# One-value-a-token rows through DRAM instead of products, in a four-layer graph network on one core

## Chip, cores and metric

One core of a Trainium2 chip runs the whole program in one launch, in float32. The metric is device microseconds of that core; on one core there is no die to compare, and all runs agree within 0.3% of their median, those of the slower kernels within 0.6%, so all are taken as of one state (the fast one). Ratios are the mean time of one kernel's runs over that of the other's of the same rounds, so not quite the ratio of the medians that are quoted. Several chips served; the kernel before took 1639.2 to 1639.6 us (median) on each, so times of different rounds may stand side by side.

## The reference, cut

```python
# x: 64 x 256 x 128, adj: 256 x 256 (one graph for all 64 items)
def layer0(x):                       # _pair_indices cut
    h = x @ others_weight
    u1, u2 = h @ a1, h @ a2          # one value a token each
    e = u1[:, idx1] + u2[:, idx2]    # leaky relu 0.1, masked by adj, softmax over axis 1
    return einsum('bik,bkl->bil', att, h) + x @ self_weight
def layer1(x):
    h = x @ W
    e = leaky_relu((h @ a_src)[:, :, None] + (h @ a_dst)[:, None, :], 0.2)  # masked, softmax over -1
    return elu(attn @ h)
x = layernorm(x + layer0(x)); x = layernorm(x + layer1(x))
x = layernorm(x + gated_5_steps(x, adj)); x = layernorm(x + chebyshev_3(x, adj))   # layers 2 and 3, cut
```

Where layers 0 and 1 need a leaky relu of "value of token i plus value of token j", one of the two must lie along the free axis of every partition: a row of 512 values (two items), the same on all 128 partitions.

## The kernel before

Two items make a unit; 32 units pass through the four layers in five lanes. All instructions are handed over in an order that a small list scheduler makes when the kernel is built; on the chip each engine then goes through its own list strictly in that order.

```python
class Plan:
    LATENCY = {"pe": 220, "dve": 150, "act": 150, "pool": 200, "sp": 3000}   # "sp": the queue of transfers
    OWN = {"pe": 0, "dve": 70, "act": 70, "pool": 100, "sp": 0}
    ...
    def seen_at(self, t, by):        # when task `by` may use what t made
        return t.end if t.eng != by.eng else t.off + self.OWN[t.eng]
    ... # run(): free[e] = t.off = now + t.ns;  t.end = t.off + self.LATENCY[e] + t.wait
```

A transfer is added with ns=450, so it is planned to land 3.45 us after its issue. Layer 0 and layer 1 before, cut:

```python
def layer0(u, L):
    xT = feature_major(u, L)                                  # 4 transposes, copy by ACT
    matmul(ps_c, wc_b, xT)                                    # the row on all partitions: 128x512   (L408)
    ... matmul(ps_d[:, b], xb[:, b, k:N:2], wu[:, k])         # one-column sums, 4                  (L412)
    ... matmul(hx[b], xb[..], wx0)                            # h and self product, 256 columns, 4  (L423)
    ... # Prelu, mask, softmax; h times 1/sum
    ... matmul(hx[b][ic, 1], p[..], h[..])                    # attention times h, 8 of 128 columns (L458)
    layernorm(...)
def layer1(u, L):
    xT = feature_major(u, L)                                  # 4 transposes
    ... matmul(ps_h[b], xb[..], wx1)                          # x W, 129 columns, 4                 (L473)
    matmul(ps_e, ws_b, xT)                                    # the row on all partitions: 128x512   (L477)
    ... # Prelu, exp, mask
    ... matmul(ps_o, p[..], h[..])                            # attention times h, 8 of 130 columns (L504)
```

The softmax here doesn't subtract the row's maximum and nothing guards it: scores larger than these inputs give would overflow.

## Time and profile before

| | kernel before |
|---|---|
| time (median) | 1639.5 us |
| span, granted TensorE clock | 1637.2 us, 0.999 |
| PE / DVE / ACT busy | 99% / 58% / 50% |
| transfers | all loads issued by 37 us; after that only the 32 stores of results |

PE is TensorE's matmuls, PEld its weight loads, DVE VectorE, ACT ScalarE, POOL GpSimd, SP the engine that issues transfers. Where PE is busy 99% of the span and every other engine at 60% or less, time is PE's sum of instructions. The lines that show it are in the prediction below.

### The profile page before, as it was taken

How to read it: one execution, taken by the hardware profiler on the slowest of the kernel's cores; microseconds unless marked ns; L12 is line 12 of the kernel's file. 1: busy time of each engine (PE TensorE's matmuls, PEld its weight loads, DVE VectorE, ACT ScalarE, POOL GpSimd, SP SyncE). 2: the span in 40 equal slices, each digit the busy share in tenths (PEclk: the TensorE clock that was granted, in tenths of full speed). 3: DMA queues.
4: the chain of work that ended last, by engine and by line, in shares of the span. 5: the costliest groups of instructions: out<-in, count | busy, mean ns of one | idle time of the engine just before them, and what ended most of it. 6: DMA issues, size and time to landing. Idle time of an engine off the chain costs nothing.

```text
span 1637.2 us, 18751 instructions
## 1 busy us (share of the span) xinstructions
PE 1615.9 (99%) x6999; PEld 1095.2 (67%) x6999; DVE 950.4 (58%) x2214; ACT 820.2 (50%) x1602; POOL 145.7 (9%) x134
## 2 busy tenths in 40 slices
PE   8899999999999999999999999999999999999998
PEld 7556667666667666676666666667666667765566
DVE  6844556655556655466555665555656556763544
ACT  4644445544554545454455544545545544654542
POOL 0100001100001100011000110001101011100001
PEclk9999999999999999999999999999999999999999
DMA  9000000000000000000000000000000000000000
GB/s 241 1 0 7 7 7 8 7 1 7 7 7 7 7 1 7 7 8 7 1 7 7 7 7 1 7 7 7 7 1 7 7 7 7 7 1 0 1 7 26
DMA packets 36731, 19.42 MB, mean 12 GB/s; under 512 B 2465, under 2 KB 36513, under 8 KB 36641
## 3 DMA queue, kind: packets, MB, share of 16 engines
q1 hardware_dynamic: 36640, 18.23, 4.2%
q8 instruction: 55, 0.90, 0.2%
q14 instruction: 36, 0.29, 0.1%
...
## 4 chain that ended last, share of the span: by engine, by line
PE 94%; DVE 3%; ACT 1%; POOL 0%; issue 0%; DMA 0%; POOLq 0%; DVEq 0%; ACTq 0%
PE ps L543 41%; PE ps L527 20%; PE ps L597 7%; PE ps L570 4%; PE ps L604 3%; PE ps L423 3%; PE ps L375 3%; PE ps L504 3%; PE ps L458 3%; PE ps L408 2%; PE ps L473 2%; PE ps L477 2%; PE ps L412 1%; DVE x L395 1%; DVE st L386 0%; POOL rstd L391 0%
## 5 line engine op out<-in xcount | busy, mean ns | idle before, releaser
L543 PE MATMUL ps<-m,gT 128*128 128x512 f32 x960 | 463.7, 595 | 1.0 <-ACT e L549 0.6
L391 POOL TENSOR_TENSOR rstd<-ve,nhalf 128x4 f32<-128x4 f32 x128 | 145.0, 1134 | 1485.7 <-DVE ve L388 1459.0
L543 PEld LDWEIGHTS ps<-m,gT 128*128 128x128 f32 x960 | 173.1, 190 | 135.3 <-issue 116.2
L527 PE MATMUL ps<-adjT,ht 128*128 128x256 f32 x1024 | 253.6, 381 | 0.5 <-ACT ht L574 0.5
L551 DVE SCALAR_TENSOR_TENSOR e<-e,xT 128x512 f32<-128x512 f32 x160 | 110.3, 690 | 205.0 <-ACT e L549 204.5
L527 PEld LDWEIGHTS ps<-adjT,ht 128*128 128x128 f32 x1024 | 188.1, 190 | 54.9 <-issue 27.4
L562 DVE TENSOR_TENSOR p<-p,xT 128x512 f32<-128x512 f32 x160 | 110.3, 689 | 175.8 <-ACT p L556 175.3
L558 ACT ACTIVATE e<-ps,bias 128x512 f32<-128x512 f32 x160 | 109.9, 687 | 146.6 <-PE ps L543 146.6
L539 ACT COPY m<-ps 128x512 f32<-128x512 f32 x160 | 93.7, 585 | 174.4 <-PE ps L527 168.8
L543 PE MATMUL ps<-xT,gT 128*128 128x512 f32 x320 | 164.2, 595 | 0.5 <-ACT xT L377 0.5
L543 PE MATMUL ps<-e,u5T 128*128 128x512 f32 x320 | 163.0, 597 | 0.9 <-DVE e L551 0.8
L549 ACT ACTIVATE e<-ps,bias 128x512 f32<-128x512 f32 x160 | 109.9, 687 | 106.7 <-PE ps L543 106.0
L527 PE MATMUL ps<-adjT,x 128*128 128x256 f32 x512 | 143.6, 380 | 0.0
L570 PEld LDWEIGHTS ps<-ident,xT 128*128 128x128 f32 x640 | 83.7, 141 | 76.6 <-issue 53.4
L556 ACT ACTIVATE p<-ps,bias 128x512 f32<-128x512 f32 x160 | 109.9, 687 | 35.2 <-PE ps L543 34.8
L574 ACT COPY ht<-ps 128x512 f32<-128x512 f32 x128 | 74.6, 585 | 97.6 <-PE ps L570 96.8
L563 DVE SCALAR_TENSOR_TENSOR p<-e,p 128x512 f32<-128x512 f32 x160 | 110.2, 689 | 21.8 <-ACT e L558 18.7
L570 PE MATMUL ps<-ident,xT 128*128 128x128 f32 x640 | 118.7, 274 | 0.6 <-DVE xT L565 0.4
L395 DVE TENSOR_SCALAR x<-ps,st,rstd 128x128 f32<-128x128 f32 x256 | 93.4, 404 | 41.6 <-POOL rstd L391 41.0
L375 PE MATMUL ps<-ident,x 128*128 128x128 f32 x512 | 112.5, 276 | 1.6 <-DVE x L395 1.1
L377 ACT COPY xT<-ps 128x512 f32<-128x512 f32 x128 | 74.6, 585 | 78.6 <-PE ps L375 78.1
L565 DVE SCALAR_TENSOR_TENSOR xT<-p,xT 128x512 f32<-128x512 f32 x160 | 110.0, 687 | 2.9
(107 smaller groups left out, 2046.4 us busy)
## 6 DMA issues: line engine op xcount, KB each, us to landing
x<-in_x_dram SPq DMA_DIRECT2D x32, 256.0 KB, 5.5
out_dram<-x SPq DMA_DIRECT2D x32, 256.0 KB, 2.3
...
adj_t<-in_adj_dram SPq DMA_DIRECT2D x1, 256.0 KB, 2.6
...
```

Source lines behind the costliest of these rows:

```text
L375: add(PE, 110, lambda g=g: nc.tensor.transpose(ps.ap[:, g * P : (g + 1) * P], X[u].ap[:, g // NC, g % NC, :], ident.ap), (X[u], ident), (ps,))
L391: add(POOL, 1050, lambda: nc.gpsimd.tensor_tensor(rstd.ap, ve.ap, nhalf.ap, op=ALU.pow), (ve, nhalf), (rstd,))
L527: add(PE, mm_ns(N), lambda b=b, mc=mc: nc.tensor.matmul(ps.ap[:, b * N : (b + 1) * N], (src.ap if len(src.ap.shape) == 4 else src.ap.rearr ...
L543: add(PE, mm_ns(T), lambda: nc.tensor.matmul(ps.ap, w(), rhs.ap, start=start, stop=stop, skip_group_check=True), (c, rhs), (ps,))
L549: add(ACT, 600, lambda ps_g=ps_g: nc.scalar.activation(r.ap, ps_g.ap, AF.Tanh, bias=bias2.ap[:, 1:2], scale=0.5), (ps_g, bias2), (r,))
L551: add(DVE, 600, lambda h=h: nc.vector.scalar_tensor_tensor(r.ap, r.ap, 1.0, h.ap, op0=ALU.add, op1=ALU.mult), (r, h), (r,))
L556: add(ACT, 600, lambda ps_v=ps_v: nc.scalar.activation(v.ap, ps_v.ap, AF.Tanh, bias=bias2.ap[:, 2:3]), (ps_v, bias2), (v,))
L562: add(DVE, 600, lambda h=h: nc.vector.tensor_sub(v.ap, v.ap, h.ap), (v, h), (v,))
L563: add(DVE, 600, lambda: nc.vector.scalar_tensor_tensor(v.ap, z.ap, 1.0, v.ap, op0=ALU.add, op1=ALU.mult), (v, z), (v,))
L565: add(DVE, 600, lambda h=h, new=new: nc.vector.scalar_tensor_tensor(new.ap, v.ap, 0.5, h.ap, op0=ALU.mult, op1=ALU.add), (v, h), (new,))
L570: add(PE, 110, lambda g=g, h=h, ps_t=ps_t: nc.tensor.transpose(ps_t.ap[:, g * P : (g + 1) * P], h.ap[:, g * P : (g + 1) * P], ident.ap), ( ...
L597: add(PE, mm_ns(N), lambda k=k, src=src, c=c, b=b: nc.tensor.matmul(view(c)[:, :, b, :], bn(src.ap)[:, b, c * P : (c + 1) * P], w3.ap[:, k ...
```

## The change

Its intent is to take products off PE. In layer 0 the row and the one-column sums come out of the h product as extra columns; in layer 1 both sums come out of layer 0's attention product as extra columns. A column has one value per partition; to turn it into a row on all partitions it is stored to DRAM and loaded back to every partition. Layer 1 multiplies attention by x first, then by W, which spares transposes and half of the products. A sixth lane is to cover the transfers; unit 0 still goes by products.

```diff
-LANES = 5
-LEAD = 20
+LANES = 6
+LEAD = 10
+DIRECT = 1
+    def to_row(row, src, col, n=1):
+        add("sp", 450, lambda: nc.sync.dma_start(
+            row.ap.rearrange("o (g p k) -> (o p) g k", g=G, k=n), src.ap[:, :, col : col + n]), (src,), (row,))
+    def from_row(t, row):
+        add("sp", 450, lambda: nc.sync.dma_start(t.ap, row.ap.rearrange("o n -> (o n)").partition_broadcast(P)), (row,), (t,))
+    def on_all(u, t, row, src, col):
+        if u >= DIRECT:
+            to_row(row, src, col); from_row(t, row); return t
+        ... # else 4 transposes of the column, broadcast
 # layer 0
-        matmul(ps_c, wc_b, xT) ... one-column sums ... h and self product, 256 columns
+        ... h product of 133 columns (h, 2 sums for layer 1, 3 for layer 0), copied early by ACT
+        to_row(L["rowu"], h, D + 2, 2); u4 <- rowu (pairs of tokens); d = u4[:, :, 0] + u4[:, :, 3]
+        row = on_all(u, lc, L["row"], h, D + 4)
+        ... self product (130 columns) and attention times h (130 columns) in one accumulation
 # layer 1
-        feature_major; x W; matmul(ps_e, ws_b, xT); attention times h
+        es = on_all(u, L["m"], L["row"], esd, 0)
+        ... ps_x = x-transposed times attention (4 of 256 columns), then W (4 of 129 columns)
 # cut: folded weights and the layernorm that goes with them, loads of x kept to two per lane, casts of views
```

`row` is 512 values of 4 bytes, `rowu` 512 pairs of 8 bytes. Each value is one piece, since a partition's four values lie apart on both sides.

More of the change, by code (lines that the diff above doesn't have):

```diff
@@ L190 @@
     PE, DVE, ACT, POOL = "pe", "dve", "act", "pool"
+    C0 = D + 5
     const = ctx.enter_context(tc.tile_pool(name="const", bufs=1))
     psum = ctx.enter_context(tc.tile_pool(name="psum", bufs=1, space=bass.MemoryType.PSUM))
+    dram = ctx.enter_context(tc.tile_pool(name="dram", bufs=1, space=bass.MemoryType.DRAM))
     def sb(name, shape):
@@ L217 @@
     out_u = out.rearrange("(u b) (c p) d -> u p b c d", b=UB, p=P)
-    X = {}
+    xs, X = [cell(f"x{k}", [P, UB, NC, D]) for k in range(2 * LANES)], {}
     def load_x(u):
-        X[u] = load(f"x{u}", x_u[u], [P, UB, NC, D], 1000)
-    adj_t = load("adj_t", adj.rearrange("(c p) j -> p c j", p=P), [P, NC, N])
+        X[u] = c = xs[u % len(xs)]
+        add("sp", 1000, lambda: nc.sync.dma_start(c.ap, x_u[u]), (), (c,))
+    w1 = load("w1", W, [D, D])
+    asd = cell("asd", [D, 2])
+    for k, a in enumerate((a_src, a_dst)):
+        add("sp", 450, lambda k=k, a=a: nc.sync.dma_start(asd.ap[:, k : k + 1], a), (), (asd,))
     wo = load("wo", others_weight, [D, D])
@@ L227 @@
     wself = load("wself", self_weight, [D, D])
+    adj_t = load("adj_t", adj.rearrange("(c p) j -> p c j", p=P), [P, NC, N])
     load_x(1)
-    w1 = load("w1", W, [D, D])
-    asd = cell("asd", [D, 2])
-    for k, a in enumerate((a_src, a_dst)):
-        add("sp", 450, lambda k=k, a=a: nc.sync.dma_start(asd.ap[:, k : k + 1], a), (), (asd,))
     load_x(2)
@@ L243 @@
     wk = load("wk", weight_1, [D, D, 7], 1500)
-    for u in range(4, NU):
+    for u in range(4, LANES):
         load_x(u)
@@ L290 @@
     add(DVE, 420, lambda: nc.vector.tensor_scalar(mask1.ap, mask1.ap, 0.0, None, op0=ALU.is_gt), (mask1,), (mask1,))
-    def projected(name, w, vecs):
-        wT = transposed(name + "T", [(w, w.ap)])
-        ps, t = bank(), cell(name, [P, 2])
-        add(PE, 150, lambda: nc.tensor.matmul(ps.ap[:, 0:2], wT.ap[:, 0], vecs.ap, start=True, stop=True),
-            (wT, vecs), (ps,))
-        add(DVE, 150, lambda: nc.vector.tensor_copy(t.ap, ps.ap[:, 0:2]), (ps,), (t,))
-        return t
-    wu = projected("wu", wo, att)
@@ L301 @@
-    wc = cell("wc", [P, 1])
-    add(DVE, 150, lambda: nc.vector.tensor_add(wc.ap, wu.ap[:, 0:1], wu.ap[:, 1:2]), (wu,), (wc,))
-    wc_b = cell("wc_b", [P, P])
-    add(DVE, 230, lambda: nc.vector.tensor_copy(wc_b.ap, wc.ap.to_broadcast([P, P])), (wc,), (wc_b,))
-    wx0 = cell("wx0", [P, 2, D])
-    add(DVE, 150, lambda: nc.vector.tensor_copy(wx0.ap[:, 0], wo.ap), (wo,), (wx0,))
-    add(DVE, 250, lambda: nc.vector.tensor_add(wx0.ap[:, 1], wself.ap, ident.ap), (wself, ident), (wx0,))
-    wsd = projected("wsd", w1, asd)
@@ L311 @@
-    ws_b = cell("ws_b", [P, P])
-    add(DVE, 230, lambda: nc.vector.tensor_copy(ws_b.ap, wsd.ap[:, 0:1].to_broadcast([P, P])), (wsd,), (ws_b,))
-    wx1 = cell("wx1", [P, D + 1])
-    add(DVE, 150, lambda: nc.vector.tensor_copy(wx1.ap[:, 0:D], w1.ap), (w1,), (wx1,))
-    add(DVE, 150, lambda: nc.vector.tensor_copy(wx1.ap[:, D : D + 1], wsd.ap[:, 1:2]), (wsd,), (wx1,))
+    centre = cell("centre", [P, P])
+    add(DVE, 150, lambda: nc.vector.tensor_scalar_add(centre.ap, ident.ap, -1.0 / D), (ident,), (centre,))
@@ new lines, in product @@
+    def product(ps, at, n, lhs, lhs_ap, rhs, rhs_ap):
+        add(PE, mm_ns(n), lambda: nc.tensor.matmul(ps.ap[:, at : at + n], lhs_ap(), rhs_ap(), start=True, stop=True,
+                                                   skip_group_check=True), (lhs, rhs), (ps,))
+    wx1 = cell("wx1", [P, D + 1])
+    w1cT = cell("w1cT", [P, D])
+    ps_w1, ps_w1T = bank(), bank()
+    product(ps_w1T, 0, D, w1, lambda: w1.ap, centre, lambda: centre.ap)
+    add(DVE, 230, lambda: nc.vector.tensor_copy(w1cT.ap, ps_w1T.ap[:, 0:D]), (ps_w1T,), (w1cT,))
@@ new lines @@
+    product(ps_w1, 0, D, centre, lambda: centre.ap, w1, lambda: w1.ap)
+    add(DVE, 230, lambda: nc.vector.tensor_copy(wx1.ap[:, 0:D], ps_w1.ap[:, 0:D]), (ps_w1,), (wx1,))
+    add(DVE, 60, lambda: nc.vector.memset(wx1.ap[:, D : D + 1], 1.0 / D), (), (wx1,))
+    right0 = cell("right0", [P, C0])
+    ps_r = bank()
+    add(DVE, 150, lambda: nc.vector.tensor_copy(right0.ap[:, 0:D], centre.ap), (centre,), (right0,))
+    product(ps_r, 0, 2, w1cT, lambda: w1cT.ap, asd, lambda: asd.ap)
+    add(DVE, 100, lambda: nc.vector.tensor_copy(right0.ap[:, D : D + 2], ps_r.ap[:, 0:2]), (ps_r,), (right0,))
@@ new lines @@
+    add(DVE, 100, lambda: nc.vector.tensor_copy(right0.ap[:, D + 2 : D + 4], att.ap), (att,), (right0,))
+    add(DVE, 100, lambda: nc.vector.tensor_add(right0.ap[:, D + 4 : D + 5], att.ap[:, 0:1], att.ap[:, 1:2]),
+        (att,), (right0,))
+    woT = transposed("woT", [(wo, wo.ap)])
+    add(DVE, 250, lambda: nc.vector.tensor_add(wself.ap, wself.ap, ident.ap), (wself, ident), (wself,))
+    wselfT = transposed("wselfT", [(wself, wself.ap)])
+    wx0, ws0 = cell("wx0", [P, C0]), cell("ws0", [P, D + 2])
@@ L318 @@
+    for t, wT, n in ((wx0, woT, C0), (ws0, wselfT, D + 2)):
+        ps = bank()
+        product(ps, 0, n, wT, lambda wT=wT: wT.ap[:, 0], right0, lambda n=n: right0.ap[:, 0:n])
+        add(DVE, 230, lambda t=t, n=n, ps=ps: nc.vector.tensor_copy(t.ap, ps.ap[:, 0:n]), (ps,), (t,))
     gs = [cell(f"gs{k}", [D, D]) for k in range(3)]
@@ L354, in lane_cells @@
             c[name] = Cell(c[at].ap.rearrange("p g n -> p (g n)")[:, half * T : (half + 1) * T])
-        c["h0"] = cell(f"h0_{k}", [P, G, D])
-        c["h1"] = cell(f"h1_{k}", [P, G, D + 2])
+        c["h0"] = cell(f"h0_{k}", [P, G, C0])
         c |= {name: cell(f"{name}_{k}", [P, G]) for name in ("nm", "s", "rs", "rstd", "ve")}
@@ L359, in lane_cells @@
         c["st"] = cell(f"st_{k}", [P, UB, 6])
-        add(DVE, 60, lambda: nc.vector.memset(c["h1"].ap[:, :, D + 1 : D + 2], 1.0), (), (c["h1"],))
+        c["u"] = cell(f"u_{k}", [P, UB, 4])
+        c["esd"] = cell(f"esd_{k}", [P, G, 2])
+        for name, n in (("row", 1), ("rowu", 2)):
+            c[name] = Cell(dram.tile([1, T * n], F32, tag=f"{name}_{k}", name=f"{name}_{k}"))
         return c
@@ L378, in feature_major, with layernorm @@
         return L[name]
-    def layernorm(u, L, pairs, swap=False):
+    def to_row(row, src, col, n=1):
[5 more added lines that the diff above has]
+        if u >= DIRECT:
+            to_row(row, src, col)
+            from_row(t, row)
+            return t
+        ps = bank()
+        for g in range(G):
+            add(PE, 110, lambda g=g: nc.tensor.transpose(
+                ps.ap[:, g * P : (g + 1) * P], src.ap[:, g, col : col + 1].to_broadcast([P, P]), ident.ap),
+                (src, ident), (ps,))
+        return ps
+    def layernorm(u, L, pairs, swap=False, centred=False):
         st, ve, rstd = L["st"], L["ve"], L["rstd"]
@@ L394, in layernorm @@
                 b, ch = (j, k) if swap else (k, j)
+                if centred:
+                    add(DVE, 260, lambda k=k, j=j, b=b, ch=ch, view=view: nc.vector.tensor_scalar(
+                        X[u].ap[:, b, ch, :], view()[:, j, :], rstd.ap[:, 2 * k + j : 2 * k + j + 1], 1.0,
+                        op0=ALU.mult, op1=ALU.add), (c, rstd), (X[u],))
+                    continue
                 add(DVE, 260, lambda k=k, j=j, b=b, ch=ch, view=view: nc.vector.tensor_scalar(
@@ L406, in layer0 @@
         xb = bn(xT.ap)
-        ps_c, ps_d = bank(), bank()
-        tail = [add(PE, mm_ns(T), lambda: nc.tensor.matmul(ps_c.ap, wc_b.ap, xT.ap, start=True, stop=True),
-                    (xT, wc_b), (ps_c,))]
+        lc, d, e, p, h, u4 = L["m"], L["d"], L["e"], L["p"], L["h0"], L["u"]
+        nm, s, rs = L["nm"], L["s"], L["rs"]
         for b in range(UB):
-            for k in range(2):
-                tail.append(add(PE, 240, lambda b=b, k=k: nc.tensor.matmul(
-                    ps_d.ap[:, b : b + 1], xb[:, b, k : N : 2], wu.ap[:, k : k + 1], start=(k == 0), stop=(k == 1)),
-                    (xT, wu), (ps_d,)))
@@ L416, in layer0 @@
-        hx = [bank() for _ in range(UB)]
-        def hxv(b):
-            return hx[b].ap.rearrange("p (c k d) -> p c k d", c=NC, k=2)
-        for b in range(UB):
-            for c in range(NC):
-                add(PE, mm_ns(N), lambda b=b, c=c: nc.tensor.matmul(
-                    hx[b].ap[:, c * N : (c + 1) * N], xb[:, b, c * P : (c + 1) * P],
-                    wx0.ap.rearrange("p k d -> p (k d)"), start=(c == 0), stop=True, skip_group_check=True),
-                    (xT, wx0), (hx[b],), tail)
@@ L427, in layer0, with hv @@
-        lc, d, nd, e, p = L["m"], L["d"], L["nd"], L["e"], L["p"]
-        nm, s, rs, h = L["nm"], L["s"], L["rs"], L["h0"]
-        add(ACT, 600, lambda: nc.scalar.activation(lc.ap, ps_c.ap, AF.Prelu, alpha=0.1), (ps_c,), (lc,))
-        add(ACT, 160, lambda: nc.scalar.activation(d.ap, ps_d.ap[:, 0:UB], AF.Prelu, alpha=0.1), (ps_d,), (d,))
+            hx = bank()
+            def hv(hx=hx):
+                return hx.ap[:, 0 : NC * C0].rearrange("p (c k) -> p c k", c=NC)
+            for c in range(NC):
+                add(PE, mm_ns(C0), lambda b=b, c=c, hv=hv: nc.tensor.matmul(
+                    hv()[:, c, :], xb[:, b, c * P : (c + 1) * P], wx0.ap, start=(c == 0), stop=True,
+                    skip_group_check=True), (xT, wx0), (hx,))
@@ new lines, in layer0 @@
+            add(ACT, 400, lambda b=b, hv=hv: nc.scalar.copy(h.ap[:, b * NC : (b + 1) * NC, :], hv()), (hx,), (h,))
+        if u >= DIRECT:
+            to_row(L["rowu"], h, D + 2, 2)
+            add("sp", 450, lambda: nc.sync.dma_start(
+                u4.ap, L["rowu"].ap.rearrange("o (b p k) -> (o p) b k", b=UB, p=P)), (L["rowu"],), (u4,))
+            add(DVE, 100, lambda: nc.vector.tensor_add(d.ap, u4.ap[:, :, 0], u4.ap[:, :, 3]), (u4,), (d,))
+            ds = d
+        else:
+            ds = bank()
+            for b in range(UB):
+                for k in range(2):
+                    add(PE, 240, lambda b=b, k=k: nc.tensor.matmul(
+                        ds.ap[:, b : b + 1], xb[:, b, k : N : 2], wx0.ap[:, D + 2 + k : D + 3 + k],
+                        start=(k == 0), stop=(k == 1)), (xT, wx0), (ds,))
@@ L431, in layer0 @@
+        add(ACT, 160, lambda: nc.scalar.activation(d.ap, ds.ap[:, 0:UB], AF.Prelu, alpha=0.1), (ds,), (d,))
+        row = on_all(u, lc, L["row"], h, D + 4)
+        add(ACT, 600, lambda: nc.scalar.activation(lc.ap, row.ap, AF.Prelu, alpha=0.1), (row,), (lc,))
         ev = e.ap.rearrange("p (b c) n -> p b c n", b=UB)
@@ L445, in layer0 @@
         for g in range(G):
-            add(ACT, 620, lambda g=g: nc.scalar.activation(
+            add(ACT, 400, lambda g=g: nc.scalar.activation(
                 p.ap[:, g, :], e.ap[:, g, :], AF.Exp, bias=nm.ap[:, g : g + 1], accum_out=s.ap[:, g : g + 1]),
                 (e, nm), (p, s))
-        add(DVE, 120, lambda: nc.vector.reciprocal(rs.ap, s.ap), (s,), (rs,))
-        for b in range(UB):
-            add(DVE, 350, lambda b=b: nc.vector.tensor_mul(
-                h.ap[:, b * NC : (b + 1) * NC, :], hxv(b)[:, :, 0, :],
-                rs.ap[:, b * NC : (b + 1) * NC].rearrange("p (c o) -> p c o", o=1).to_broadcast([P, NC, D])),
-                (hx[b], rs), (h,))
@@ L455, in layer0, with yv @@
-        for b in range(UB):
+        tail = [add(DVE, 120, lambda: nc.vector.reciprocal(rs.ap, s.ap), (s,), (rs,))]
+        add(DVE, 700, lambda: nc.vector.tensor_mul(
+            h.ap[:, :, 0 : D + 2], h.ap[:, :, 0 : D + 2],
+            rs.ap.rearrange("p (g o) -> p g o", o=1).to_broadcast([P, G, D + 2])), (h, rs), (h,))
+        esd, rstd = L["esd"], L["rstd"]
+        ys = []
+        for b in range(UB):
+            y = bank()
+            def yv(y=y):
+                return y.ap[:, 0 : NC * (D + 2)].rearrange("p (c k) -> p c k", c=NC)
+            ys.append((y, yv))
+            for c in range(NC):
+                add(PE, mm_ns(D + 2), lambda b=b, c=c, yv=yv: nc.tensor.matmul(
+                    yv()[:, c, :], xb[:, b, c * P : (c + 1) * P], ws0.ap, start=(c == 0), stop=False,
+                    skip_group_check=True), (xT, ws0), (y,), tail)
@@ L456, in layer0 @@
             for ic in range(NC):
                 for kc in range(NC):
-                    add(PE, mm_ns(P), lambda b=b, ic=ic, kc=kc: nc.tensor.matmul(
-                        hxv(b)[:, ic, 1, :], p.ap[:, b * NC + kc, ic * P : (ic + 1) * P], h.ap[:, b * NC + kc, :],
-                        start=False, stop=True, skip_group_check=True), (p, h), (hx[b],))
-        layernorm(u, L, [(hx[b], lambda b=b: hxv(b)[:, :, 1, :]) for b in range(UB)])
-    def layer1(u, L):
-        xT = feature_major(u, L)
-        xb = bn(xT.ap)
-        H = D + 2
-        ps_h = [bank() for _ in range(UB)]
-        tail = []
-        for b in range(UB):
-            for c in range(NC):
-                tail.append(add(PE, mm_ns(D + 1), lambda b=b, c=c: nc.tensor.matmul(
-                    ps_h[b].ap[:, c * H : c * H + D + 1], xb[:, b, c * P : (c + 1) * P], wx1.ap,
-                    start=(c == 0), stop=True, skip_group_check=True), (xT, wx1), (ps_h[b],)))
-        ps_e = bank()
-        add(PE, mm_ns(T), lambda: nc.tensor.matmul(ps_e.ap, ws_b.ap, xT.ap, start=True, stop=True),
-            (xT, ws_b), (ps_e,), tail)
-        h, e, p = L["h1"], L["e"], L["p"]
-        for b in range(UB):
-            add(ACT, 300, lambda b=b: nc.scalar.copy(
-                h.ap[:, b * NC : (b + 1) * NC, 0 : D + 1],
-                ps_h[b].ap[:, 0 : NC * H].rearrange("p (c k) -> p c k", c=NC)[:, :, 0 : D + 1]), (ps_h[b],), (h,))
@@ new lines, in layer0 @@
+                    add(PE, mm_ns(D + 2), lambda b=b, ic=ic, kc=kc, yv=yv: nc.tensor.matmul(
+                        yv()[:, ic, :], p.ap[:, b * NC + kc, ic * P : (ic + 1) * P], h.ap[:, b * NC + kc, 0 : D + 2],
+                        start=False, stop=(kc == NC - 1), skip_group_check=True), (p, h), (y,))
+        layernorm(u, L, [(y, lambda yv=yv: yv()[:, :, 0:D]) for y, yv in ys], centred=True)
+        for b, (y, yv) in enumerate(ys):
+            add(DVE, 120, lambda b=b, yv=yv: nc.vector.tensor_mul(
+                esd.ap[:, b * NC : (b + 1) * NC, :], yv()[:, :, D : D + 2],
+                rstd.ap[:, b * NC : (b + 1) * NC].rearrange("p (c o) -> p c o", o=1).to_broadcast([P, NC, 2])),
+                (y, rstd), (esd,))
@@ L484, in layer1 @@
+    def layer1(u, L):
+        H = D + 1
+        esd, e, p = L["esd"], L["e"], L["p"]
+        es = on_all(u, L["m"], L["row"], esd, 0)
         for g in range(G):
@@ L486, in layer1 @@
             add(ACT, 400, lambda g=g, b=b: nc.scalar.activation(
-                e.ap[:, g, :], ps_e.ap[:, b * N : (b + 1) * N], AF.Prelu, bias=h.ap[:, g, D : D + 1], alpha=0.2),
-                (ps_e, h), (e,))
+                e.ap[:, g, :], bn(es.ap)[:, b, :], AF.Prelu, bias=esd.ap[:, g, 1:2], alpha=0.2), (es, esd), (e,))
         ef, pf = e.ap.rearrange("p g n -> p (g n)"), p.ap.rearrange("p g n -> p (g n)")
@@ L493, in layer1 @@
             mask1.ap.rearrange("p (o c) n -> p o (c n)", o=1).to_broadcast([P, UB, NC * N])), (e, mask1), (p,))
+        ps_x, px = bank(), L["xT0"]
+        for b in range(UB):
+            for jc in range(NC):
+                add(PE, mm_ns(N), lambda b=b, jc=jc: nc.tensor.matmul(
+                    ps_x.ap[:, b * N : (b + 1) * N], X[u].ap[:, b, jc, :], p.ap[:, b * NC + jc, :],
+                    start=(b == 0 and jc == 0), stop=(jc == NC - 1), skip_group_check=True), (X[u], p), (ps_x,))
+        add(ACT, 500, lambda: nc.scalar.copy(px.ap, ps_x.ap), (ps_x,), (px,))
         rs, hp, hn, th = L["rs"], L["ht"], L["m"], L["xT1"]
-        ex = Cell(L["h0"].ap.rearrange("p g d -> p (g d)"))
+        ex = L["h0"]
+        exf = ex.ap.rearrange("p g d -> p (g d)")[:, 0:T]
         for b in range(UB):
@@ L502, in layer1 @@
             for ic in range(NC):
-                for jc in range(NC):
-                    add(PE, mm_ns(H), lambda b=b, ic=ic, jc=jc, ov=ov: nc.tensor.matmul(
-                        ov()[:, ic, :], p.ap[:, b * NC + jc, ic * P : (ic + 1) * P], h.ap[:, b * NC + jc, :],
-                        start=(ic == 0 and jc == 0), stop=True, skip_group_check=True), (p, h), (ps_o,))
+                add(PE, mm_ns(H), lambda b=b, ic=ic, ov=ov: nc.tensor.matmul(
+                    ov()[:, ic, :], bn(px.ap)[:, b, ic * P : (ic + 1) * P], wx1.ap,
+                    start=(ic == 0), stop=True, skip_group_check=True), (px, wx1), (ps_o,))
             r = rs.ap[:, b * NC : (b + 1) * NC].rearrange("p (c o) -> p c o", o=1)
-            add(DVE, 120, lambda r=r, ov=ov: nc.vector.reciprocal(r, ov()[:, :, D + 1 : D + 2]), (ps_o,), (rs,))
+            add(DVE, 120, lambda r=r, ov=ov: nc.vector.reciprocal(r, ov()[:, :, D : D + 1]), (ps_o,), (rs,))
             add(DVE, 350, lambda b=b, r=r, ov=ov: nc.vector.tensor_mul(
@@ L513, in layer1 @@
         add(ACT, 550, lambda: nc.scalar.activation(th.ap, hn.ap, AF.Tanh, scale=0.5), (hn,), (th,))
-        add(ACT, 550, lambda: nc.scalar.activation(ex.ap, hn.ap, AF.Exp), (hn,), (ex,))
+        add(ACT, 550, lambda: nc.scalar.activation(exf, hn.ap, AF.Exp), (hn,), (ex,))
         xf = X[u].ap.rearrange("p b c d -> p (b c d)")
@@ L517, in layer1 @@
             (hp, X[u]), (hp,))
-        add(DVE, 600, lambda: nc.vector.scalar_tensor_tensor(th.ap, ex.ap, 1.0, th.ap, op0=ALU.add, op1=ALU.mult),
+        add(DVE, 600, lambda: nc.vector.scalar_tensor_tensor(th.ap, exf, 1.0, th.ap, op0=ALU.add, op1=ALU.mult),
             (ex, th), (th,))
@@ L610, in spawn @@
     def spawn(u, lane):
+        if u + LANES < NU:
+            load_x(u + LANES)
         for layer in (layer0, layer1, layer2, layer3):
```

## The prediction

> **What bounds the kernel now.** I read the page first, its busy table and its chain that ended last.
>
> ```profile
> PE 1615.9 (99%) x6999; PEld 1095.2 (67%) x6999; DVE 950.4 (58%) x2214; ACT 820.2 (50%) x1602; POOL 145.7 (9%) x134
> ...
> PE 94%; DVE 3%; ACT 1%; POOL 0%; issue 0%; DMA 0%; POOLq 0%; DVEq 0%; ACTq 0%
> ```
>
> TensorE (PE) works 99% of the span, and the chain from the last instruction back to the first runs over PE for 94% of it. VectorE (DVE) and ScalarE (ACT) have 40% and more in hand. A busy PE could still be a PE that drags, so I next asked what one product costs from one start to the next. The timeline of 700 to 720 us has nearly every shape of the kernel in it; its columns are start, length in us, engine, line and how many.
>
> ```profile
> 708.84 1.89 PE L597 MATMUL ps<-w,m 128*128 128x256 f32 x8
> 710.57 1.02 PE L543 MATMUL ps<-m,gT 128*128 128x512 f32 x2
> 711.42 1.89 PE L604 MATMUL ps<-e,a2T 128*128 128x256 f32 x8
> 713.15 1.02 PE L543 MATMUL ps<-e,u5T 128*128 128x512 f32 x2
> 714.01 1.05 PE L473 MATMUL ps<-wx,xT 128*128 128x129 f32 x8
> 714.90 1.02 PE L477 MATMUL ps<-xT,ws_b 128*128 128x512 f32 x2
> 715.76 1.95 PE L458 MATMUL ps<-h,p 128*128 128x128 f32 x16
> 717.61 0.30 PE L570 MATMUL ps<-ident,xT 128*128 128x128 f32 x1
> ...
> 718.93 1.00 PE L412 MATMUL ps<-wu,xT 128*128 128x1 f32 x8
> 719.80 0.46 PE L527 MATMUL ps<-adjT,ht 128*128 128x256 f32 x1
> ```
>
> Take starts, not lengths: a row's length overlaps the next row. From 708.84 to 710.57 eight instructions of 256 columns pass, 216 ns each; a pair of 512 takes 0.86 us (714.90 to 715.76), 430 ns each; eight of 129 take 0.89 us, 111 ns each; sixteen of 128 take 1.85 us, 116 ns; eight of ONE column still take 0.87 us, 109 ns. There is no gap between rows. So PE's time is a ledger: count instructions, multiply by the price of their shape. An f32 product is two instructions in this trace (160 steps with 5 products of 512 columns are 1600 instructions on L543), a transpose is one, of 109 ns.
>
> Last I looked for where PE does not run back to back: the table by stretch (PE busy is the figure after "20.00,") and the waits of PE (total us, times, longest).
>
> ```profile
> 0.00:20.00 20.00, 16.13 (x78) 13.33 (x79) 11.39 (x45) 7.07 (x18) 0.70 (x6) 1.00 0.90 242
> 20.00:40.00 20.00, 19.27 (x126) 16.31 (x126) 16.06 (x56) 12.70 (x43) 3.04 (x3) 1.00 1.05 251
> 40.00:60.00 20.00, 16.59 (x110) 13.04 (x109) 12.15 (x36) 13.14 (x32) 2.01 (x2) 1.00 0.00 1
> 60.00:80.00 20.00, 18.36 (x85) 11.22 (x84) 20.00 (x54) 12.45 (x23) 5.18 (x4) 1.00 0.00 1
> 80.00:100.00 20.00, 20.00 (x75) 12.31 (x74) 7.95 (x16) 10.03 (x17) 0.78 (x1) 1.00 0.00 1
> ```
>
> ```profile
> PE ps L504 <- DVE p L491: 3.2, 3, 1.2
> ```
>
> About 10 us of PE idleness lie in the first 80 us (3.9 + 0.7 + 3.4 + 1.6), where all five lanes are in layers 0 and 1 together and DVE is full (20.00 of 20 in 60 to 80); the largest single cause is layer 1's masking on DVE. After that PE is full until the last seven us, which are the last layernorm and store.
>
> **What the Trainium skill says.** (1) "FP8 and Floating Point Precision", section TensorE Precision Notes, has true FP32 as four passes through the array. The trace agrees in price: a 512-column product costs 0.86 us, four times 512 columns at 2.4 GHz (0.853 us), as two instructions of two passes. (2) "TensorE: Matmul & The Clock Gate", section LDWEIGHTS (loading the stationary operand), gives columns/1.2 ns for a weight load, 107 ns for 128 columns, whatever is streamed. The trace agrees: 109 ns is the floor of a one-column product. (3) The same page, Part 1, says an idle PE falls to half clock after about 3.4 us and needs as long to recover. The chain shows the cold price at the start: 8 instructions of 256 columns in 3.62 us, 452 ns each against 216 later.
>
> ```profile
> 5.76 3.62 PE ps L343 x8
> ```
>
> (4) "DMA: Bandwidth & Descriptors", section Latency and other measured facts, puts most of a transfer's fixed cost of about 2 us into the receipt from memory, HBM worst. The trace agrees: stores of 256 KB land 2.3 us after issue.
>
> ```profile
> out_dram<-x SPq DMA_DIRECT2D x32, 256.0 KB, 2.3
> ```
>
> Nothing there or in the trace prices a store of 512 separate 4-byte values, which the change needs.
>
> **The change part by part.** A unit is two batch items; 32 units pass. First PE, per unit, in us, prices as above (130 columns: 53.02 to 54.80 us in the timeline, 16 in 1.78).
>
> Removed. Layer 0: the row on all partitions as a product with a replicated vector, L408, 0.86; the one-column sums of L412, 8 x 109 = 0.87; h and self product at 256 columns, L423, 8 x 216 = 1.73; attention times h, L458, 1.85. Layer 1: feature-major transposes, 4 x 109 = 0.44; x times W, L473, 0.89; the row product L477, 0.86; attention times h, L504, 1.78. Sum 9.28.
>
> Added. Layer 0: x times the wider weight (133 columns), 8 x 113 (2 x 133/2.4 + 2.5) = 0.91; self product at 130 columns, 8 x 111 = 0.89; attention times h at 130 columns, 1.78. Layer 1: attention times x, four products of 256 columns, 8 x 216 = 1.73; then W, 8 of 129 columns, 0.89. Sum 6.20.
>
> The reason layer 1 wins: attention times x comes out feature-major, so W follows at four products, where attention times h needed eight with a weight load each, plus the transposes. The saving is 3.08 us per unit, 98.6 us for 32. Unit 0 alone still goes through products (some 1.8 us more), so 97 us net, all of it on the engine that sets the end.
>
> The instruction listing of the two kernels agrees with the count: 198 products fewer on PE (2984 against 3182), +3 on ACT, +70 on DVE, +186 on the DMA issuer, which is six transfers for each of 31 units.
>
> Other engines, per unit. DVE was 950.4/32 = 29.7; it loses two multiplies of 0.42, gains one of 520 columns (about 0.70), two small ones of 0.16 and an add of 0.15: 30.0, or 62% of a new period of 48 us. ACT was 25.6; it loses one copy of 0.59 and two of 0.38, gains two of about 0.38 and one of 0.59: unchanged, 53%. The DMA issuer: 0.43 to 0.5 us an issue, some 3.6 us per unit.
>
> Latency. Each round trip through DRAM is two landings, about 5 us; a unit has one in layer 0 (both rows side by side) and one in layer 1, 10 us more in a life of 5 x 51 = 253 us before. Six lanes give a unit 6 x 48 = 290 us. So the sixth lane pays for the round trips several times over, and these units are the youngest, whose products fill what older ones leave. In the middle I expect PE to stay full. The banks of layer 0, formerly held from the product to the layernorm, are freed by an early copy, which helps too.
>
> Start. Here I expect to give some back: all lanes begin with layers 0 and 1, which now hold less PE work but as much DVE work, and the rows wait for DRAM. Also the first wide weight now needs a_dst, which is the twentieth issue of the queue and behind nearly 3 MB of other loads (at the 242 GB/s of the first stretch, about 12 us), so products on x can't begin before 14 to 16 us. On the other side unit 0 reaches layer 2 sooner. An idle PE of over 3 us also cools its clock. I put the sum at +5 us, between 0 and 20.
>
> Sum: 1639.5 - 97 + 5 = 1547.
>
> **The rivals.** (A) The ledger alone, with gaps unchanged: 1542, or 1532 if freer banks and the sixth lane close some of the gaps. For it: PE gaps after 80 us are nearly nil. (B) The wait that replaces: each engine's order is fixed at build, so a row that lands late stops ACT's Prelu, and behind it the tanh of older units. If 1 us is exposed twice for each of 31 units, 62 us of the gain go and the time is near 1605; with 4-byte stores at two or three times the usual landing it is likely somewhere in part. Against it: the order was built with 3.45 us for a transfer, above the 2.3 us that stores show, and ACT has slack. (C) DVE becomes the bound at the start for longer: up to 20 us, 1562. (D) The store of single values clogs the queue: 1024 tiny pieces per unit and layer 0 over 16 engines; I think it small, as loads of 512 pieces of 512 B took 31 ns a piece.
>
> **Range and chances.** Centre 1547. Low end 1530 from A with better gaps; high end 1570 from B in part or C in full. Slower than 1607 would need B in full; over 1672 I see no way but a serialised queue. Faster by over 2%: 0.95, within 2%: 0.04, slower: 0.01.
>
> **What would show each step right or wrong.** PE busy near 1520 us and still 98% or more; the layer 1 group of attention times x at 256 instructions of 216 ns, and no group of transposes or 512-column rows in layers 0 and 1. DVE at 62%, ACT at 53%. Waits of PE in the first 80 us of 10 to 25 us, released by DVE, ACT or a_dst's load. Waits of ACT on the row's load short in the middle. I am wrong if the row's store lands in over 4 us, if ACT's waits on DMA reach tens of us and PE waits on ACT follow, or if PE falls below 96%.

## The result

The changed kernel takes 2150.55 us (2148.6 to 2152.8, 4 runs), 1.312 times the time before (95%: 1.309 to 1.314). The forecast was 1547. The results are correct, and all runs agree.

The page of the changed kernel: busy times, the chain that ended last by engine and by line, and the granted clock in 40 slices (tenths of full speed).

```profile
PE 1649.3 (77%) x6509; PEld 1093.8 (51%) x6509; DVE 951.3 (44%) x2274; ACT 819.8 (38%) x1602; POOL 142.0 (7%) x134
...
PEclk7689999789998979898989899878998778879999
...
PE 49%; DMA 37%; DVE 6%; ACT 5%; issue 1%; SPq 1%; POOL 1%; POOLq 0%; ACTq 0%; DVEq 0%
PE ps L606 26%; DMA row<-esd 13%; DMA row<-h 12%; PE ps L590 10%; DMA m<-row 9%; PE ps L660 3%; PE ps L633 2%; PE ps L667 2%; DMA rowu<-h 2%; PE ps L553 1%; ACT e L542 1%; PE ps L523 1%; PE ps L567 1%; PE ps L396 1%; POOL rstd L435 1%
```

DMA, nearly absent from the chain before (0%), now makes 37% of it: the two stores of `row` and the load of it. DVE and ACT are busy for as long as foreseen (951 and 820 us); they are not the bound. Where did 604 us over the forecast go? PE idles 2149.8 - 1649.3 = 500 us, against 21 before and some 26 forecast: +474. And PE is busy 1649 us where the ledger gave 1615.9 - 97 = 1519: +130. Nearly all of that is the clock (mean 0.878): the trace has it at half speed behind PE's pauses (59 of over 1 us, the longest 24.7), for 494 of the 6509 instructions, and these took 123 us longer than their price at full clock (the prices under The experiments). Together 604.

What a transfer takes from issue to landing, in the list of DMA issues (how many, KB, median us):

```profile
m<-row SPq DMA_DIRECT2D x62, 256.0 KB, 4.7
x<-in_x_dram SPq DMA_DIRECT2D x32, 256.0 KB, 2.8
out_dram<-x SPq DMA_DIRECT2D x32, 256.0 KB, 2.3
rowu<-h SPq DMA_DIRECT2D x31, 4.0 KB, 4.2
row<-h SPq DMA_DIRECT2D x31, 2.0 KB, 9.4
u<-rowu SPq DMA_DIRECT2D x31, 4.0 KB, 5.0
row<-esd SPq DMA_DIRECT2D x31, 2.0 KB, 9.6
```

The store of 2 KB in 512 pieces of 4 bytes takes four times as long as the store of 256 KB. Of the 31 `row<-esd`, 20 were issued with no other transfer in flight; they took 8.2 us at the shortest and 8.7 as a median, so most of this is not a matter of what lies ahead in the queue. The load to all partitions takes 4.7. A round trip is 14 us, not 5.

A stretch of the chain shows how that reaches PE (start, length, what):

```profile
997.53 0.27 ACT h L468
...
997.82 0.36 SPq L403
...
998.22 8.46 DMA row<-h
...
1006.76 4.82 DMA m<-row
...
1011.60 0.63 ACT m L485
1012.23 0.49 ACT p L501 x2
1012.72 0.58 ACT e L612
...
1013.35 2.08 PE ps L606 x2
```

ACT copies the h product, which holds the column, at 997.5; the store takes 8.5 us, the load 4.8; ACT stands at the Prelu of this row (L485) until 1011.6, and only behind it in its list comes the tanh L612 of an older unit in layer 2, on which PE's next product waits. This is rival B of the prediction, at several times the size it was given. ACT's longest waits say the same (total us, times, longest):

```profile
ACT e L542 <- DMA m<-row: 268.5, 31, 12.7
ACT m L485 <- DMA m<-row: 220.4, 31, 12.5
```

Now the queue of transfers itself, 22 to 51 us, in the timeline:

```profile
21.87 0.37 SPq L403 DMA_DIRECT2D rowu<-h  x1
22.28 0.51 SPq L403 DMA_DIRECT2D row<-h  x1
26.31 0.36 SPq L472 DMA_DIRECT2D u<-rowu  x1
30.90 0.33 SPq L408 DMA_DIRECT2D m<-row  x1
31.32 0.39 SPq L403 DMA_DIRECT2D rowu<-h  x1
31.76 0.50 SPq L403 DMA_DIRECT2D row<-h  x1
41.40 0.36 SPq L472 DMA_DIRECT2D u<-rowu  x1
```

After the store of unit 2's row at 31.76 nothing is issued for 9.1 us (32.26 to 41.40): the next in the list is a load of what that queue has just stored, and it must wait for the landing; everything behind it waits as well. The trace of the first 160 us has PE busy for only 75 us (150 before); from 40 to 60 us it does nothing and its clock falls to 0.56 (the figure before the last two):

```profile
40.00:60.00 20.00, 0.00 (x0) 0.00 (x0) 3.74 (x14) 1.33 (x4) 1.18 (x1) 0.56 0.38 27
```

### The profile page after: what moved, and what is told of

Its sections match the earlier page's. It is cut to its first block, busy times and chain, and to the rows that moved or that the text cites. A ratio compares the mean times of both kernels' runs of the same rounds, so it can differ in the third digit from the quotient of the medians. Undisturbed runs are those within 1.5% of the kernel's fastest.

```text
span 2149.8 us, 18061 instructions
## 1 busy us (share of the span) xinstructions
PE 1649.3 (77%) x6509; PEld 1093.8 (51%) x6509; DVE 951.3 (44%) x2274; ACT 819.8 (38%) x1602; POOL 142.0 (7%) x134
## 4 chain that ended last, share of the span: by engine, by line
PE 49%; DMA 37%; DVE 6%; ACT 5%; issue 1%; SPq 1%; POOL 1%; POOLq 0%; ACTq 0%; DVEq 0%
PE ps L606 26%; DMA row<-esd 13%; DMA row<-h 12%; PE ps L590 10%; DMA m<-row 9%; PE ps L660 3%; PE ps L633 2%; PE ps L667 2%; DMA rowu<-h 2%; PE ps L553 1%; ACT e L542 1%; PE ps L523 1%; PE ps L567 1%; PE ps L396 1%; POOL rstd L435 1%
## 5 line engine op out<-in xcount | busy, mean ns | idle before, releaser
L606 PE MATMUL ps<-m,gT 128*128 128x512 f32 x960 | 507.8, 643 | 181.6 <-ACT m L602 130.1
L606 PEld LDWEIGHTS ps<-m,gT 128*128 128x128 f32 x960 | 182.3, 205 | 318.5 <-ACT m L602 140.4
L590 PE MATMUL ps<-adjT,ht 128*128 128x256 f32 x1024 | 272.0, 398 | 47.5 <-ACT ht L637 47.4
L590 PEld LDWEIGHTS ps<-adjT,ht 128*128 128x128 f32 x1024 | 197.3, 199 | 125.1 <-ACT ht L637 57.1
L606 PE MATMUL ps<-xT,gT 128*128 128x512 f32 x320 | 178.7, 643 | 53.3 <-ACT xT L398 48.1
L606 PE MATMUL ps<-e,u5T 128*128 128x512 f32 x320 | 170.9, 622 | 0.0
L542 ACT ACTIVATE e<-m,esd 128x256 f32<-128x256 f32 x124 | 57.0, 500 | 268.5 <-DMA m<-row 268.5
L612 ACT ACTIVATE e<-ps,bias 128x512 f32<-128x512 f32 x160 | 109.8, 686 | 111.5 <-PE ps L606 111.4
L633 PE MATMUL ps<-ident,xT 128*128 128x128 f32 x640 | 128.3, 282 | 12.7 <-DVE xT L628 12.6
L553 PE MATMUL ps<-p,x 128*128 128x256 f32 x256 | 73.1, 409 | 49.9 <-DVE p L546 49.9
L660 PE MATMUL ps<-w,xT 128*128 128x256 f32 x256 | 71.2, 414 | 45.6 <-ACT xT L398 45.6
```

The costliest lines, as they stand in the source:

```text
L590: add(PE, mm_ns(N), lambda b=b, mc=mc: nc.tensor.matmul(ps.ap[:, b * N : (b + 1) * N], (src.ap if len(src.ap.shape) == 4 else src.ap.rearr ...
L606: add(PE, mm_ns(T), lambda: nc.tensor.matmul(ps.ap, w(), rhs.ap, start=start, stop=stop, skip_group_check=True), (c, rhs), (ps,))
L612: add(ACT, 600, lambda ps_g=ps_g: nc.scalar.activation(r.ap, ps_g.ap, AF.Tanh, bias=bias2.ap[:, 1:2], scale=0.5), (ps_g, bias2), (r,))
L633: add(PE, 110, lambda g=g, h=h, ps_t=ps_t: nc.tensor.transpose(ps_t.ap[:, g * P : (g + 1) * P], h.ap[:, g * P : (g + 1) * P], ident.ap), ( ...
L660: add(PE, mm_ns(N), lambda k=k, src=src, c=c, b=b: nc.tensor.matmul(view(c)[:, :, b, :], bn(src.ap)[:, b, c * P : (c + 1) * P], w3.ap[:, k ...
```

## The experiments

"PE gaps" below are distances from one PE start to the next less the price of the shape (2 x columns/2.4 + 2.5 ns, at least 109 ns), summed over the trace. They are 35 us in the kernel before and 641 us in the changed one. Instructions at these prices sum to 1592 us before and to 1499 us in the changed kernel.

| kernel | us | ratio to before |
|---|---|---|
| changed | 2150.6 | 1.312 |
| all_products | 1596.6 | 0.974 |
| true_latencies | 2109.7 | 1.288 |
| row_by_partition | 2058.1 | 1.256 |
| row_sixteen_bytes | 1756.8 | 1.072 |
| order_knows_landing | 2037.1 | 1.241 |
| order_knows_true | 1856.8 | 1.133 |
| sixteen_knows | 1620.9 | 0.989 |
| sixteen_generous | 1619.2 | 0.988 |
| layer1_rows_only | 1595.7 | 0.973 |
| sixteen_start6 | 1595.5 | 0.973 |
| layer1_rows_start6 | 1603.6 | 0.978 |
| products_five_lanes | 1617.7 | 0.987 |
| changed_start6 | 2055.5 | 1.254 |
| all_stores_wide | 1584.8 | 0.967 |
| start6_generous | 1587.8 | 0.969 |
| wide_generous | 1578.4 | 0.963 |

All give correct results.

### all_products: no row through DRAM

```diff
-DIRECT = 1
+DIRECT = 32
```

> All units take the way of unit 0: the rows reach the partitions through transposes and one-column sums, nothing goes through DRAM; six lanes, the new layer 1 and the stagger stay. Theory 1 (the loss is only the late rows): PE's ledger grows by 31 x 1.74 = 54 us over the predicted one, the waits of ACT on a row vanish, the clock is back at 1.0 and the time is 1590 to 1615 us. Theory 2 (the sixth lane, the stagger or the new start lose the time): it stays above 1700 us.

Measured: 1596.6 us, theory 1. The page:

```profile
PE 1572.5 (99%) x7005; PEld 1084.5 (68%) x7005; DVE 944.2 (59%) x2243; ACT 815.0 (51%) x1602; POOL 144.2 (9%) x134
```

PE's busy time differs from the kernel before by 1572.5 - 1615.9 = -43.4 us; the prediction's ledger with products for all units is -97 + 54 = -43. That they agree to the microsecond is partly luck: at the prices of the shapes the two traces differ by 39 us (1592 and 1553). The ledger was right within some 4 us, the new layer 1 is worth its products, and the whole loss comes with the rows through DRAM.

### true_latencies: the scheduler gets the measured landings

```diff
-... src.ap[:, :, col : col + n]), (src,), (row,))
+... src.ap[:, :, col : col + n]), (src,), (row,), wait=6100 if n == 1 else 800)
 # likewise wait=1300 for the load to all partitions, 1600 for u4's
```

> The same instructions as the changed kernel; only the figures with which the order is built are the measured landings: row store 9.5 us instead of 3.45, row to all partitions 4.7, the other store 4.2, its load 5.0. Theory 1a (what hurts is that the fixed order counts on rows that come 6 us later): 1545 to 1620 us, landings unchanged at 9.5 us. Theory 1b (two round trips of 14 us are simply too long for six lanes): above 1800 us.

Measured: 2109.7 us. My theory 1a fell: a right figure for the landing gained 2%. The time lies where theory 1b put it, but the trace shows another reason. The queue's timeline looked as before, a load next behind its store, the same stand of 9 us, and in all the queue waited as long for its own stores (568 us, 569 in the changed kernel). The reason is `seen_at`: for two tasks of one engine it counts the first as done when it is issued, and adds 70 ns for ACT or DVE and nothing for a transfer. To the scheduler, store and load of a row took 0.45 + 0.45 + 3.0 = 3.9 us together (5.2 here, with the load's own wait), whatever landing the store was given.

### order_knows_landing and order_knows_true: the same line mended, without and with the figures

```diff
-        return t.end if t.eng != by.eng else t.off + self.OWN[t.eng]
+        return t.end if t.eng != by.eng or t.eng == "sp" else t.off + self.OWN[t.eng]
```

> true_latencies fell flat, and its trace says why: the order still issues the load of a row 0.45 us behind its own store, for the builder takes a transfer as done for another transfer when it is issued, if both are of the same queue. On the chip the queue stands until the store has landed and everything behind stands with it. Here one line lets a transfer wait for the landing of another (planned 3.45 us); nothing else differs from the changed kernel. Theory 3 (the queue that stands is what loses the time): a large part comes back though the stores really take 9.5 us: 1620 to 1850 us. Theory 1b (the round trips are too long for six lanes): it stays above 2000 us.

Measured: 2037.1 us. That is 113 us less than the changed kernel, far from theory 3's range and, by the mark of 2000 us set beforehand, on the side of theory 1b. A load is now listed 3.45 us behind its store, and the store takes 10; the queue still waited 527 us for its own stores.

> order_knows_landing together with the measured landings of true_latencies: store 9.5 us, load 4.7, the other store 4.2, its load 5.0. Theory 3: the queue hardly stands any more, 1565 to 1650 us, PE 96% or more, with landings as slow as in the changed kernel. Theory 1b: above 1900 us. If it is between, something else in the transfers, such as several in flight slowing each other, is left.

Measured: 1856.8 us, between the theories, and 294 us off the changed kernel by order alone. The figures gave 41 us without the line, the line 113 without the figures, both together 294. The queue at the start now issues the stores of four units in a row:

```profile
21.89 0.37 SPq L403 DMA_DIRECT2D rowu<-h  x1
22.30 0.51 SPq L403 DMA_DIRECT2D row<-h  x1
22.91 0.45 SPq L403 DMA_DIRECT2D rowu<-h  x1
...
23.95 0.44 SPq L403 DMA_DIRECT2D row<-h  x1
24.49 0.45 SPq L403 DMA_DIRECT2D rowu<-h  x1
```

But the landings grow when several are in flight: of those that this trace resolves, the load to all has a median of 11.1 us (4.7 in the changed kernel), `row<-h` 12.1, the longest 36. It looks as if transfers queue behind the slow stores; then a fixed figure per transfer can't be right for them, and the order goes wrong again wherever they meet. The queue still waited 430 us for its own stores here. Whether theory 1b (round trips too long for six lanes) has a part in what is left is not shown: quick stores, below, make the same order work, but they shorten the round trip as well, and no run keeps the slow stores with more lanes.

### row_by_partition and row_sixteen_bytes: what makes the store slow

```diff
 # row_by_partition: position p*G + g in DRAM; readers take the row with a step of 4 values
-            row.ap.rearrange("o (g p k) -> (o p) g k", g=G, k=n), ...
+            row.ap.rearrange("o (p g k) -> (o p) g k", g=G, k=n), ...      # for n == 1
 # row_sixteen_bytes: besides, the source lies side by side: esd as [P, 2, G]; DVE copies the column of h to [P, 1, G]
```

> The row lies in DRAM by partition instead of by group, so that the four values of a partition stand side by side: still 512 pieces of 4 bytes, but a run of eight partitions now owns 128 bytes alone instead of 32 between its neighbours. If neighbouring writers in one stretch of memory make the store slow, it lands in 4.5 us or less, and the time is 1600 to 1850 us. If the width of a piece, 4 bytes, makes it slow, it lands in 9 us or more and the time stays near 2150 us.

> As row_by_partition, with sources that lie side by side too, so that the store is 128 pieces of 16 bytes (one small copy on DVE a unit more). By either cause of the slow store it now lands in 2 to 3.5 us. The load to all partitions still takes 4.7 us against the planned 3.45. Time 1560 to 1750 us; if the store still lands in 9 us, neither piece width nor neighbours are the cause.

Measured: 2058.1 us with the store landing in 7.4 (esd) and 7.9 us (h), median, shortest 6.4: neither of the two outcomes that were expected. And 1756.8 us, 7 us over its range, with 2.4 and 3.1 us, shortest 1.4. Neighbours in memory are a small part (8.2 to 6.4); the many 4-byte pieces are the large one. In numbers of the traces, the landing of a store that is issued with no other transfer in flight, shortest and median: 512 pieces of 4 bytes 8.2 and 8.7 us, 512 of 8 bytes (`rowu`) 2.9 and 3.4, 128 of 16 bytes 1.4 and 1.4. Number alone does not explain it (4 against 8 bytes at the same number), nor bytes alone; why is left open. The 394 us from 2150.6 to 1756.8 are the price of the pieces, their neighbours included, under the old order, a little more even, since both variants slow ACT: layer 1's Prelu, which reads the row with a step of 16 bytes, takes 742 ns (row_by_partition) in place of 500, ACT's busy time rises by 40 us. Both also load layer 0's row into another tile than before; what that alone does was not run.

### sixteen_knows and sixteen_generous: quick stores and the mended order

```diff
 # row_sixteen_bytes with the mended seen_at; wait=300 (load to all), 800 (store of rowu), else 0
 # sixteen_generous: wait=2500 for every row transfer
```

> row_sixteen_bytes with an order that knows that a load waits for its store's landing, and landings as that run measured them: 3.45 us for the store, 3.75 for the load to all, 4.25 and 3.45 for the other pair. Theory 3: 1545 to 1580 us, PE 98%, ACT's waits for rows under 30 us in all; faster than both kernels. Otherwise it stays above 1650 us.

> As sixteen_knows with landings planned 2.5 us longer than 3.45 each, so that nearly every real landing is earlier than planned. If what is left after the mended order is the spread of the landings (a late one stalls ACT), this is faster than sixteen_knows by 5 to 30 us; if not, it is 0 to 20 us slower, for units live longer.

Measured: 1620.9 and 1619.2 us. Both beat the kernel before by 1% (clear of the noise, though less than the 2% that the record calls faster), neither reaches 1580; the two can't be told apart. The order is worth 136 us with quick stores, and the queue's waits for its own stores fall from 212 us to 111. PE gaps are 113 and 109 us; 42 of the first fall in the first 80 us, where eight stores of four units are issued within five microseconds (22.5 to 27.2 us) and land one behind the other, the `rowu` of 26.0 us only after 11.9 us. The spread of landings is not the main rest here (later, with products at the start, planning for it brings 8 us).

### layer1_rows_only, sixteen_start6, layer1_rows_start6: fewer transfers, or a start without them

```diff
 # sixteen_start6: sixteen_knows with
-DIRECT = 1
+DIRECT = 6
 # layer1_rows_only: sixteen_knows, layer 0's row and sums by products in all units; layer1_rows_start6: both
```

> sixteen_knows with layer 0 by products (transposes and one-column sums, 31 x 1.31 = 41 us more of PE than the changed kernel) and only layer 1's row through DRAM: two transfers a unit instead of six. If what is left in sixteen_knows (1621 us against a ledger of 1545) comes from many transfers sharing one queue, above all the two stores of layer 0, the gaps shrink to those of all_products and the time is 1575 to 1592 us. If any row through DRAM costs its share, it is 1605 us or more.

> sixteen_knows with products for the first six units in place of the first one: 5 x 1.74 = 9 us more on PE, but no ten stores of small pieces one behind the other at the start, where that run's PE gaps are 42 us in the first 80 us against 15 in the kernel before. If the burst at the start is the cause of these gaps, the time falls to 1598 to 1612 us; if not, it rises by 5 to 10 us.

> Both: layer 1's row through DRAM, from the seventh unit on. Expected 1572 to 1590 us, the best of all if both reasons hold; the start then has no row transfer at all.

Measured: 1595.7, 1595.5 and 1603.6 us. The burst at the start is confirmed: sixteen_start6 gains 25 us, a little more than expected, though PE has 9 us more to do, and its gaps in the first 80 us fall from 42 to 16, those of the kernel before (15). layer1_rows_only lands just over its range: the gaps shrink to 45 us, and its saving on PE over all_products (products of one row, 31 x 0.44 = 14 us) is used up by them. layer1_rows_start6 is a miss: 8 us slower than without the six units, of which PE's added products are 2; the rest I can't explain.

### products_five_lanes: what the sixth lane is for

```diff
 # all_products with
-LANES = 6
-LEAD = 10
+LANES = 5
+LEAD = 20
```

> all_products with five lanes and the stagger of the kernel before (20). The sixth lane was thought to hide the round trips; without any round trip it should matter little: 1595 to 1608 us. If the sixth lane itself fills PE's gaps, the time is over 1610 us.

Measured: 1617.7 us, out of its range and over the 1610 that would speak for the sixth lane. Six lanes with stagger 10 are worth 21 us where there is no round trip to hide at all: the gaps fall from 55 us to 32. Lane and stagger were changed together, and which of them does it is open.

### changed_start6: the changed kernel's own start

```diff
-DIRECT = 1
+DIRECT = 6
```

> The changed kernel as it is, four-byte stores and its own order, with products for the first six units. The changed kernel loses 101 us of PE in its first 160 us against some 15 in the kernel before. If the loss is made alike at the start and in the middle by the same transfers, this gives back 60 to 90 us: 2060 to 2090 us. Much more would mean that the late start drags on for the rest of the run.

Measured: 2055.5 us, 95 less (60 to 90 were expected), about the 101 us of PE gaps that the changed kernel has in its first 160 us. The rest of the loss is made in the middle, some 12 us in every 40.

### all_stores_wide, start6_generous, wide_generous: what is left

```diff
 # all_stores_wide: sixteen_start6; DVE copies three columns of h to c4 [P, 3, G]; the sums are stored side by side
+            L["rowu"].ap.rearrange("o (p w) -> (o p) w", w=2 * G), c4.ap[:, 0:2, :]      # 128 pieces of 32 bytes
 # start6_generous: sixteen_start6 with wait=2500 for every row transfer; wide_generous: both
```

> sixteen_start6 with the last store of small pieces gone too: the two sums of a token are copied side by side first, so that this store is 128 pieces of 32 bytes in place of 512 of 8 (its load is two transfers of 64 pieces). If the width and number of pieces set how long a store keeps the queue, it lands in about 1.5 us instead of 3.9, the PE gaps after 80 us shrink from 60 us to 20 to 40, and the time is 1560 to 1585 us. If the gaps come from the number of transfers, not from their pieces, it stays at 1590 to 1600 us.

> sixteen_start6 with every row transfer planned 2.5 us longer than 3.45 us, so that nearly every landing is early. If the gaps left in the middle come from landings later than planned, they shrink and the time is 1575 to 1590 us; if not, it stays within 6 us of 1595.

> all_stores_wide and start6_generous together: wide pieces in every store, products for six units, an order that waits for landings and plans each row transfer 2.5 us over 3.45. Each alone took 8 to 11 us off sixteen_start6 (1595.5); if they take the same gaps, this stays at 1583 to 1588 us, if different ones, it is 1572 to 1580 us. The ledger of PE for it is about 1508 us plus 10 at the two ends.

Measured: 1584.8, 1587.8 and 1578.4 us. The wide store lands in 1.4 us (3.9 before) and gains 11 us, though PE's gaps after 80 us only fall from 60 to 49 us (20 to 40 were expected); the early plan gains 8, both 17 of the 19 that they would bring if apart. So the rest had both causes, and they overlap a little. wide_generous is 3.7% faster than the kernel before (0.963, 95%: 0.961 to 0.965), the best of all. Its page:

```profile
PE 1539.0 (98%) x6589; PEld 1041.0 (66%) x6589; DVE 951.3 (60%) x2321; ACT 852.1 (54%) x1602; POOL 141.1 (9%) x134
...
PE 86%; ACT 8%; DVE 5%; issue 1%; POOL 0%; DMA 0%; SPq 0%; POOLq 0%; DVEq 0%; ACTq 0%
```

DMA is gone from the chain again, and the queue waited 27 us for its own stores. PE gaps are 59 us, against 32 in all_products and 35 before. Of its 61 us over the kernel before, all_products has 43 without any row through DRAM; the rows in their best form bring the other 18.

## Why the prediction was wrong, point by point

**Bound and ledger: right.** PE is the bound before, and the change takes work off it: at the prices of the shapes the two traces differ by 93 us (1592 and 1499), 4 less than forecast; most of that is the product of 128 columns, put at 116 ns from one stretch, where the price has 109 and the median of the trace is 112. Three readings on the way were off and cost nothing: the listing's "198 products fewer" is not what the traces show (6999 and 6509 instructions on PE, 490 fewer, and 60 more on DVE); PE's longest wait in the first 80 us was for the load of `adj` (3.5 us), ahead of layer 1's masking (3.2); and 5 x 51 is 255, 6 x 48 is 288.

**Latency: the step that failed.** The prediction had "each round trip through DRAM is two landings, about 5 us" and "in the middle I expect PE to stay full". Measured: 9.5 us for the store and 4.7 for the load, 14 us, and a PE that is busy 77% of the span. The figure for a store of 4-byte pieces was taken from stores of 256 KB, although the prediction itself said that nothing in trace or skill prices such a store; an unknown was filled with the nearest number. The shapes that the trace before does show, loads of 4-byte pieces and stores of 512-byte pieces, don't tell it.

**Rival B: the right mechanism, dismissed by a wrong argument.** "Against it: the order was built with 3.45 us for a transfer, above the 2.3 us that stores show". Both halves failed. The true figure was above the planned one; and the plan didn't use its figure between a store and its load at all, since `seen_at` lets a transfer follow another of its queue at issue. That line stood in the kernel before, where no transfer depended on another and it did no harm. I read the figure and not the line that uses it. The queue waited 569 us for its own stores (sum of these lines):

```profile
SPq L408 <- DMA row<-esd: 282.2, 31, 13.6
...
SPq L408 <- DMA row<-h: 153.8, 29, 10.4
SPq L472 <- DMA rowu<-h: 132.7, 31, 9.1
```

"Trainium skill, DMA: Bandwidth & Descriptors", section Rules for kernel authors, says it outright: a transfer that reads what another wrote has to wait for the other's completion before it is issued, and sharing the queue does not order them. The trace agrees: 31.76 to 41.40 us above.

**Rival D: set aside too early.** It named the tiny pieces, and called them small because "loads of 512 pieces of 512 B took 31 ns a piece". The pieces turned out to be the largest single term: 394 us by row_sixteen_bytes.

**Range.** B "in full" was put at 1605 us, with 1 us exposed twice a unit. The waits of ACT on rows alone come to 489 us over 62 waits, 7.9 us each. Two errors that multiply, a fourfold landing and an order that makes the queue stand, were not in any rival. The prediction did name "a serialised queue" as the only way over 1672 us; it gave that no cost, and any slower time a chance of 0.01, and this is what came. All three of its signs of being wrong came too: a row's store over 4 us (9.5), ACT's waits on DMA at tens of us with PE waiting on ACT (489), and PE below 96% (77).

**Start: right in kind, wrong in size.** +5 us, 0 to 20, was forecast, the rows' wait for DRAM included; it was some 100 us of PE gaps in the first 160 us. Without the rows, in all_products, 13 us of gaps lie in the first 80 us, less than before.

**Clock.** The prediction named the cooling and left it out of the middle; it is 123 us of PE's busy time here.

**How the loss comes apart.** 2150.6; with 16-byte pieces 1756.8; with an order that waits for landings 1620.9; with products at the start 1595.5; with the last store wide 1584.8; planned with a margin 1578.4. In the other sequence the order and true figures come first, 1856.8, and the pieces then give 236. So the terms depend on their order, but the first three are each shown by a run that undoes it alone (row_sixteen_bytes, order_knows_true, changed_start6).

What stays open: why 4-byte pieces take some two and a half times as long as as many of 8 bytes; whether six lanes are too few for round trips of 14 us; the 27 us of gaps more than in all_products that the best version still has; why layer1_rows_start6 is slower than layer1_rows_only; whether lane or stagger makes the 21 us.

## What to carry to other kernels

Before a value goes through DRAM, time that very transfer, with its pieces: here 2 KB in pieces of 4 bytes took four times as long as 256 KB, and putting a partition's values side by side first (a copy of 0.16 us) was worth 394 us under the old order. When an order is fixed at build, look at how the builder counts a dependence inside one queue; a transfer is done when it lands, and a queue whose next entry waits for a landing holds up all that follows. A removal of work from the busiest engine shows in the time only if what replaces it can't stop that engine's feeders: nearly the same saving gave +31% in one form and -3.7% in another.

## What the Trainium skill lacked or had wrong

- "DMA: Bandwidth & Descriptors" (Specifications; Why small descriptors are slow) says that pieces below 512 bytes cost bandwidth and read-modify-write, but gives no time to landing for a store of many small pieces; its fixed cost of some 2 us does not hold there. Runs, shortest and median with no other transfer in flight: 512 x 4 bytes 8.2 and 8.7 us, 512 x 8 bytes 2.9 and 3.4, 128 x 16 bytes 1.4 and 1.4.
- The same page (Latency and other measured facts) counts the receipt from memory within that fixed cost of about 2 us. For the store of 998.22 us most 4-byte records lie before 999.7 us and the last before 1003, each 7 to 28 ns long, and the landing at 1006.7: at least 3.7 us later, which no packet record shows.
- The same page has no figure for a load of one 2 KB row to 128 partitions: 3.0 us at the shortest, 4.7 as a median, against 2.8 for a load of 256 KB.
- "SBUF — State Buffer", which tells of 16-byte lines and a penalty for each new line, gives no figure for ScalarE: a Prelu of 256 float32 read with a step of 16 bytes took 742 ns against 500, one of 512 took 1108 against 629 (row_by_partition against the changed kernel).
